# Attention scores half a key tile ahead, in the beats in which layer 1 has no step in flight

## The chip, the cores and the metric

The kernel runs on one core of a Trainium2 chip, as one launch. The metric is the device time of that launch in microseconds. The kernel before took 4408.22 us, the median of three runs (4399.3, 4408.22 and 4410.45).

## What is computed

Two layers of attention over a graph of N = 2048 nodes with F = 256 features, for a batch of B = 8, all in fp32. Layer 0 is four-headed attention (head size 64) in which the scores are clipped to ±10, an edge that is missing counts as -10, and the softmax is taken over each chunk of 256 keys on its own and the chunks' results are added. Layer 1 is a graph attention layer of one head over the layer-0 output. Both are followed by a residual sum and a layer normalisation. Cut to what matters here:

```python
scores = einsum('bhnd,bhjcd->bhnjc', q, kc) / sqrt(Dh)      # layer 0
scores = clip(scores, -10.0, 10.0)
scores = where(mask == 0, -10.0, scores)
attn = softmax(scores, axis=-1)                             # over the 256 keys of a chunk
ctx = einsum('bhnjc,bhjcd->bhnd', attn, vc)
out = ctx @ Wo.T + bo
...
e = leaky_relu(s_i[:, :, None] + s_j[:, None, :], 0.2)      # layer 1
e = where(mask, e, -inf)
h_prime = softmax(e, axis=-1) @ Wh
```

## The kernel before

**Beats.** The program is one long list of beats, and each engine gets its instructions in the order in which the beats write them down; nothing reorders them afterwards. For each batch element b there are four blocks of 512 queries (ib), and for each block 16 key tiles of 128 (c). One beat is one key tile of one block, so there are 16 × 4 × 8 = 512 beats, and behind them a tail in which layer 1 of the last batch element finishes. Two beats are a chunk (J counts chunks; half is 0 or 1 in it).

**What a beat holds for layer 0 (lines 880 to 978).** The two head pairs (hp 0 and 1) each get a score tile `sc` of 128 keys × 2 heads × 512 queries, that is 4 KB in each partition, or two banks of PSUM. TensorE writes both (line 904), VectorE clips both against the mask in place (line 914), ScalarE takes the exponential of both into SBUF tiles `e` (line 917), which sets the place in PSUM free. Then comes the product with the values for the chunk before (`prev`): the sums of the softmax ("part 2", with a matrix of ones) and the first half of each head's values ("part 0") in the beat of half 0, the second half ("part 1") in the beat of half 1 (line 933). Each part goes to a place of 2 KB, `m`, from which ScalarE copies it to SBUF: `ds` (line 947) for the sums, `un` (line 941) for the values. From `ds` a transfer makes a small tile `dc`, VectorE takes its reciprocal (line 955), two more transfers spread it to `r`, VectorE multiplies (lines 966 and 968) and GpSimd adds into `ctxT` (line 969).

**What surrounds it.** `begin_beat` writes ScalarE's and VectorE's part of layer 1, `end_beat` its product on TensorE (line 746) and then one step of each of the generators in flight: the projections, the masks (in the first batch element alone: lines 154 to 161 and 201), the end of a layer-0 block (`fin`: the product `po`, two normalisations, the transposes `pt`), the preparation of layer 1 (`prelude`: `pw`, `psj`, the row maxima at line 438, the transposes `pab`), and the end of a layer-1 block (`fin1`). After the beat c = 15 the next block's queries are projected (`pq`, line 256).

**PSUM.** Three pools fill its 16 KB in each partition: `ps_s` has two places of 4 KB (tag `sc`), `ps_u` has one of 4 KB, which holds layer 1's sums (`us`), and `ps_m` has two of 2 KB, tag `m`, which all the short-lived tiles share in turn: `m` of the value products, `pk`, `pv`, `pq`, `po`, `pt`, `pw`, `psj`, `pab`. A tile that takes a place waits until what held it before has been read.

**Where layer 1 rests.** Layer 1 of a batch element can only start when layer 0 of that element is done, and takes fewer beats than layer 0. So there is a stretch in each batch element without any step of layer 1. With `b`, `ib` and `c` counted through, these are the beats 0 to 88, and then 19 beats (from c = 6 of the first block to c = 8 of the second) of each of the elements 2 to 7, from 134, 198, 262, 326, 390 and 454 on: 203 of 512 beats. The name `spare` (line 898) tells of them. In these beats each third score tile goes into the place of `ps_u`, so that scores have three places in turn; in all other beats they have the two of `ps_s`.

Of the kernel before, what the change touches and what calls it, by code (L numbers as in the profile page):

```python
# [9 lines left out]
F32 = mybir.dt.float32  # L10
# [3 lines left out]
AF = mybir.ActivationFunctionType  # L14
# [5 lines left out]
P = 128  # L20
CLIP = 10.0
# [7 lines left out]
def tile_adj_attention__then__gat(  # L29
# [108 lines left out]
    def mask_block(n, ib, hf, name):  # L138
        t = two.tile([P, HT, IB], I8, tag=f"mask{n}", name=f"mk{n}_{name}")
        nc.sync.dma_start(out=t, in_=mask[n][ib, hf])  # L140
        return t
# [21 lines left out]
    def masks_made():  # L163


        for ib in range(NIB):
            for hf in range(2):
                first = (ib, hf) == (0, 0)
                while not first and beat < HT * (2 * ib + hf - 1):
                    yield  # L170
                if first:
                    raw, m0 = first_raw, first_m0
                else:
                    raw = one.tile([P, HT, IB], I32, tag="wh", name=f"raw{ib}_{hf}")
                    m0 = two.tile([P, HT, IB], I8, tag="mask0", name=f"mk0_0_{ib}_{hf}")
                    blocks0[ib, hf] = m0
                m1 = two.tile([P, HT, IB], I8, tag="mask1", name=f"mb1_{ib}_{hf}")
                for i in range(HT // 2 + 2):
                    if first:
                        if 0 < i < HT // 2:  # L180
                            make_mask(0, m0, raw, ib, hf, 2 * i, 2)
                    elif i < HT // 2:
                        load_raw(raw, ib, hf, 2 * i, 2)
                    if i >= 2:
                        if not first:
                            make_mask(0, m0, raw, ib, hf, 2 * i - 4, 2)
                        make_mask(1, m1, raw, ib, hf, 2 * i - 4, 2)
                    if i or not first:
                        yield
                nc.sync.dma_start(out=mask[0][ib, hf], in_=m0)  # L190
                nc.sync.dma_start(out=mask[1][ib, hf], in_=m1)
# [667 lines left out]


    first_m0 = two.tile([P, HT, IB], I8, tag="mask0", name="mk0_0_0_0")
    blocks0 = {(0, 0): first_m0}
    make_kT(0, 0)
    make_mask(0, first_m0, first_raw, 0, 0, 0, 2)
    qT = make_qT(0, 0, xT_kv[0, 0])
# [4 lines left out]

    prev = None
    halves_done = 0
    mk0 = {}
    for J in range(total + 1):
        b, ib, j = J // (NIB * NCH), J // NCH % NIB, J % NCH
        live = J < total
# [3 lines left out]
        for half in range(2):  # L880
            c = 2 * j + half
            if live:

                if c % HT == 0:
                    if b == 0:
                        mk = blocks0[ib, c // HT]
                    else:
                        mk = mk0.pop((b, ib, c // HT))
                if c % HT == 1:
                    n = (b * NIB + ib) * 2 + c // HT + 1  # L890
                    nb, nib, nhf = n // (2 * NIB), n // 2 % NIB, n % 2
                    if 0 < nb < B:
                        mk0[nb, nib, nhf] = mask_block(0, nib, nhf, f"{nb}_{nib}_{nhf}")
            begin_beat(RATE if b < B - 1 else LAST_RATE)
            if live:
                scs = []

                spare = not (l1_open() or leaking)
                for hp in range(NPAIR):
                    pool, tag = (ps_u, "us") if spare and halves_done % 3 == 2 else (ps_s, "sc")  # L900
                    halves_done += 1
                    sc = pool.tile([P, 2, IB], F32, tag=tag, name=f"sc{b}_{ib}_{c}_{hp}")
                    for h in range(2):
                        nc.tensor.matmul(  # L904
                            sc[:, h, :],
                            kTs[b][c // TPB][h * D : (h + 1) * D, hp, ts(c % TPB, P)],
                            qT[h * D : (h + 1) * D, hp, :],
                            start=True,
                            stop=True,
                        )  # L910
                    scs.append(sc)
                cap = mk[:, c % HT, :].unsqueeze(1).to_broadcast([P, 2, IB])
                for hp in range(NPAIR):
                    nc.vector.scalar_tensor_tensor(scs[hp], scs[hp], -CLIP, cap, ALU.max, ALU.min)  # L914
                for hp in range(NPAIR):
                    e = eight.tile([P, 2, IB], F32, tag="e", name=f"e{b}_{ib}_{c}_{hp}")
                    nc.scalar.activation(e, scs[hp], AF.Exp)  # L917
                    cur["es"].append(e)
            middle_of_beat()

            early = J < NIB * NCH
            if prev is not None:
                if half == 0:

                    pool, tag = (one, "hr") if early and J % 3 == 2 else (two, "un")
                    prev["un"] = pool.tile([P, 2, IB], F32, tag=tag, name=f"un{prev['name']}")
                for part in ((2, 0), (1,))[half]:
                    m = ps_m.tile([P, IB], F32, tag="m", name=f"u{prev['name']}_{part}")
                    for i in range(2):
                        pc = 2 * prev["j"] + i  # L930
                        for h in range(H):
                            f0 = h * D + part * DH
                            nc.tensor.matmul(  # L933
                                m[h * DH : (h + 1) * DH, :],
                                prev["v"][pc // TPB][:, pc % TPB, f0 : f0 + DH] if part < 2 else ones[:, 0:DH],
                                prev["es"][2 * i + h // 2][:, h % 2, :],
                                start=(i == 0),
                                stop=(i == 1),
                            )
                    if part < 2:  # L940
                        nc.scalar.copy(prev["un"][:, part, :], m)  # L941
                    else:

                        ds = two.tile([P, IB], F32, tag="ds", name=f"ds{prev['name']}")
                        nc.scalar.copy(ds, m)  # L947
                        dc = two.tile([P, IB // DH], F32, tag="dc", name=f"dc{prev['name']}")
                        nc.sync.dma_start(
                            out=dc, in_=ds.rearrange("(h m) (n w) -> h m n w", m=DH, n=DH)[:, 0, :, :]  # L950
                        )
                        prev["dc"] = dc

                        def inverse(p=prev):
                            nc.vector.reciprocal(p["dc"], p["dc"])  # L955
                            p["rd"] = dram3.tile([H, IB], F32, tag="rd", name=f"rd{p['name']}")
                            nc.sync.dma_start(out=p["rd"].rearrange("h (m w) -> (h m) w", m=DH), in_=p["dc"])

                        def spread(p=prev):
                            p["r"] = two.tile([P, IB], F32, tag="r", name=f"r{p['name']}")  # L960
                            nc.sync.dma_start(out=p["r"], in_=p["rd"].unsqueeze(1).to_broadcast([H, DH, IB]))

                        def scaled(p=prev):
                            r2 = p["r"].unsqueeze(1).to_broadcast([P, 2, IB])
                            if p["j"] == 0:
                                nc.vector.tensor_mul(p["ctxT"], p["un"], r2)
                            else:
                                nc.vector.tensor_mul(p["un"], p["un"], r2)  # L968
                                nc.gpsimd.tensor_add(p["ctxT"], p["ctxT"], p["un"])  # L969
                            if p["j"] == NCH - 1:  # L970
                                ctx_done[p["b"], p["ib"]] = beat
                            if p["j"] == NCH - 3:
                                fins.append(fin(p["b"], p["ib"], p["ctxT"]))

                        lag = 1 if early else 0
                        at(beat + lag, inverse)
                        at(beat + lag, spread)
                        at(beat + 2 + 2 * lag, scaled)

            end_beat()  # L980
            if half == 1:

                if live and j == NCH - 2 and J + 2 < total:
                    nb, nib = (b, ib + 1) if ib + 1 < NIB else (b + 1, 0)
                    xq = xT_tile(nb, nib, "q")
                if live and j == NCH - 1 and J + 1 < total:
                    qT = make_qT(nb, nib, xq)
            beat += 1
# [51 lines left out]
```

## Time and profile before

The profile is that of one execution, which took 4410.7 us; the span of its instructions is 4408.9 us.

| | |
|---|---|
| median of three runs | 4408.22 us |
| the profiled execution, and its span | 4410.7 us, 4408.9 us |
| mean granted TensorE clock | 0.976 |
| busy: TensorE, VectorE, ScalarE, GpSimd | 92%, 77%, 58%, 40% |
| score matmuls (line 904) | 1049.1 us over 4096 |
| clip (line 914) | 1206.8 us over 1024, 1222 ns each |
| exponential (line 917) | 1035.2 us over 1024, 1021 ns each |
| value products (line 933), values and sums | 984.8 us and 497.0 us |
| copies `un` and `ds` (lines 941 and 947) | 587 ns and 580 ns each |

How to read the profile: for each instruction it has the start, the time it took, the engine, the line of the code, what it writes and reads (out<-in), and how long the engine had been idle before it and which instruction ended that idle time. A TensorE instruction has two rows, the load of its weights (PEld) and the matmul itself (PE); a score or value matmul in fp32 shows as two. Where a group of instructions of one kind is merged, the time is that of the whole group and the idle time that before its first.

### The profile page before, as it was taken

To read this page: it belongs to the slowest core of one execution; us is meant where nothing else is said; L and a number is where in the kernel's file an instruction comes from. 1 tells how busy PE (TensorE), PEld (TensorE's weight loads), DVE (VectorE), ACT (ScalarE), POOL (GpSimd) and SP (SyncE) were. 2 spreads that over 40 slices of the span, in tenths; PEclk is the share of its full clock that TensorE was granted. 3 is DMA by queue.
4 is the path that set the end of the run, shared out by engine and by line. 5 is a ranking of instruction groups with operands and counts; after the bars stand their busy time and mean duration, and the time that the engine had idled before them with its cause. 6 is when DMAs were issued, how large, how long until landed. Compare 5 with 4: busy or idle time off the path is not lost. (4 is left out here: it accounts for less than half of the span.)

```text
span 4408.9 us, 61096 instructions
## 1 busy us (share of the span) xinstructions
PE 4071.0 (92%) x23053; PEld 1917.2 (43%) x23053; DVE 3414.9 (77%) x4530; ACT 2563.4 (58%) x3842; POOL 1762.7 (40%) x901
## 2 busy tenths in 40 slices
PE   8889989999899999999899998999989999899767
PEld 3223334454344533444344543445434454344456
DVE  5876589965898659986699766996579965888777
ACT  5655556665566556665556655566556665555546
POOL 0222235542455434444245442554325542355420
PEclk9999999999999999999999999999999999999889
DMA  5554232222322233321333223222232222322321
GB/s 162 171 173 143 78 109 90 80 75 85 102 88 82 64 106 96 98 77 51 105 100 104 73 72 106 82 93 81 70 104 85 90 76 66 116 79 80 125 75 58
DMA packets 257641, 415.62 MB, mean 94 GB/s; under 512 B 85441, under 2 KB 120513, under 8 KB 256449
## 3 DMA queue, kind: packets, MB, share of 16 engines
q1 hardware_dynamic: 257344, 411.71, 30.7%
q8 instruction: 181, 2.97, 0.3%
q14 instruction: 116, 0.94, 0.1%
HBM read 340.66 MB, written 68.88 MB: 93 GB/s over the span
## 5 line engine op out<-in xcount | busy, mean ns | idle before, releaser
L917 ACT ACTIVATE e<-sc 128x1024 f32<-128x1024 f32 x1024 | 1035.2, 1021 | 1059.5 <-DVE sc L914 1018.0
L914 DVE SCALAR_TENSOR_TENSOR sc<-sc,mk 128x1024 f32<-128x1024 f32 x1024 | 1206.8, 1222 | 545.4 <-PE sc L904 357.5
L904 PE MATMUL sc<-qT,kT 64*128 64x512 f32 x4096 | 1049.1, 628 | 61.8 <-ACT e L917 58.5
L969 POOL TENSOR_TENSOR ctxT<-ctxT,un 128x1024 f32<-128x1024 f32 x224 | 569.3, 2542 | 1169.1 <-DVE un L968 1032.0
L933 PE MATMUL u<-e,v 128*32 128x512 f32 x8192 | 984.8, 598 | 3.3 <-ACT ds L947 3.2
L746 PE MATMUL us<-wh,w 128*128 128x256 f32 x3584 | 880.0, 395 | 83.2 <-ACT w L727 60.2
L746 PEld LDWEIGHTS us<-wh,w 128*128 128x128 f32 x3584 | 667.7, 193 | 425.0 <-ACT w L727 111.7
L736 POOL TENSOR_TENSOR acc<-acc,w 128x512 f32<-128x512 f32 x392 | 602.0, 1536 | 544.9 <-ACT w L727 534.3
L904 PEld LDWEIGHTS sc<-qT,kT 64*128 64x128 f32 x4096 | 349.1, 189 | 574.0 <-issue 369.0
L718 DVE SCALAR_TENSOR_TENSOR w<-ab,sj,w 128x512 f32<-128x512 f32 x512 | 571.7, 1138 | 6.2 <-ACT w L714 6.2
L933 PEld LDWEIGHTS u<-e,v 128*32 128x32 f32 x8192 | 240.6, 110 | 665.7 <-issue 541.5
L933 PE MATMUL u<-e,ones 128*32 128x512 f32 x4096 | 497.0, 603 | 0.0
L723 DVE TENSOR_TENSOR w<-w,mk 128x512 f32<-128x512 f32 x512 | 458.0, 915 | 38.3 <-DMA mk<-mask 35.7
L438 DVE CUSTOM_DVE_ANT_0 fb<-sj_row,fb 128x1024 bf16<-128x1024 f32 x240 | 381.8, 1601 | 4.2 <-DMA fb<-far 4.2
L714 ACT ACTIVATE w<-ab,sj 128x512 f32<-128x512 f32 x512 | 352.1, 714 | 10.2 <-POOL acc L734 5.4
L727 ACT ACTIVATE w<-w 128x512 f32<-128x512 f32 x512 | 308.8, 629 | 76.8 <-DVE w L723 76.4
L941 ACT COPY un<-u 128x512 f32<-128x512 f32 x512 | 300.8, 587 | 66.4 <-PE u L933 58.3
L968 DVE TENSOR_TENSOR un<-un,r 128x1024 f32<-128x1024 f32 x224 | 277.4, 1239 | 45.0 <-DMA r<-rd 44.8
L933 PEld LDWEIGHTS u<-e,ones 128*32 128x32 f32 x4096 | 107.5, 110 | 353.8 <-issue 300.5
L955 DVE RECIPROCAL dc<-dc 128x16 f32<-128x16 f32 x256 | 63.6, 249 | 156.6 <-DMA dc<-ds 141.1
L357 PE MATMUL po<-WT_o,ctxT 128*128 128x256 f32 x512 | 121.6, 391 | 30.6 <-POOL ctxT L969 23.2
L947 ACT COPY ds<-u 128x512 f32<-128x512 f32 x256 | 148.5, 580 | 1.6 <-PE u L933 1.6
(112 smaller groups left out, 3097.7 us busy)
## 6 DMA issues: line engine op xcount, KB each, us to landing
r<-rd SPq DMA_DIRECT2D x256, 256.0 KB
mk<-mask SPq DMA_DIRECT2D x120, 512.0 KB
fb<-far SPq DMA_DIRECT2D x240, 256.0 KB
xT_k<-in_xT_dram SPq DMA_DIRECT2D x32, 512.0 KB
raw<-in_adjT_dram SPq DMA_DIRECT2D x32, 512.0 KB
rawf<-in_adj_dram SPq DMA_DIRECT2D x32, 512.0 KB
x<-in_x_dram SPq DMA_DIRECT2D x32, 512.0 KB
h_d<-y SPq DMA_DIRECT2D x32, 512.0 KB
```

The costliest lines, as they stand in the source:

```text
L438: nc.vector.tensor_tensor_reduce(out=fb, in0=row, in1=fb, scale=1.0, scalar=2 * FAR * 0.999, op0=ALU.add, op1=ALU.max, accum_out=dst,)
L714: nc.scalar.activation(self.w, k["ab"][:, 1, :], AF.Identity, bias=k["sj"][:, 1, c : c + 1])
L718: nc.vector.scalar_tensor_tensor(self.w, k["ab"][:, 0, :], k["sj"][:, 0, c : c + 1], self.w, ALU.add, ALU.max)
L723: nc.vector.tensor_tensor(self.w, self.w, self.k["mks"][self.c // HT][:, self.c % HT, :], ALU.min)
L727: nc.scalar.activation(self.w, self.w, AF.Exp)
L736: nc.gpsimd.tensor_add(k["acc"], k["acc"], self.w)
L746: nc.tensor.matmul(k["us"][:, t, :], self.w[:, ts(t, P)], k["wh"][c // TPB][:, c % TPB, 0:F], start=(first and t % 2 == 0), stop=last, ski ...
L904: nc.tensor.matmul(sc[:, h, :], kTs[b][c // TPB][h * D : (h + 1) * D, hp, ts(c % TPB, P)], qT[h * D : (h + 1) * D, hp, :], start=True, sto ...
L914: nc.vector.scalar_tensor_tensor(scs[hp], scs[hp], -CLIP, cap, ALU.max, ALU.min)
L917: nc.scalar.activation(e, scs[hp], AF.Exp)
L933: nc.tensor.matmul(m[h * DH : (h + 1) * DH, :], prev["v"][pc // TPB][:, pc % TPB, f0 : f0 + DH] if part < 2 else ones[:, 0:DH], prev["es"] ...
L969: nc.gpsimd.tensor_add(p["ctxT"], p["ctxT"], p["un"])
```

## The change

In a beat in which layer 1 rests, the scores written are no longer those of the two head pairs of tile c, but the second head pair of tile c and the first of tile c + 1. Their clips follow in that order. Of the exponentials, that of (c, 0), whose score was clipped in the beat before, is written at the head of the beat, ahead of `begin_beat`; that of (c, 1) follows the clips; that of (c + 1, 0) is left for the next beat. A block's first tile has nothing ahead, so the beat c = 0 writes three scores and three clips, and c = 15 one of each. The same holds where a rest begins (three) and behind its end (one), and at one tile of the very first block (c = 7 to 8), whose mask is made only just before. The masks of layer 0 are looked up by tile in one table instead of being fetched once in half a block. The number of matmuls, clips, exponentials and transfers is unchanged, and so are the three places and the rule that hands them out.

```diff
-                for hp in range(NPAIR):
-                    pool, tag = (ps_u, "us") if spare and halves_done % 3 == 2 else (ps_s, "sc")
-                    halves_done += 1
-                    sc = pool.tile([P, 2, IB], F32, tag=tag, name=f"sc{b}_{ib}_{c}_{hp}")
...
-                    scs.append(sc)
-                cap = mk[:, c % HT, :].unsqueeze(1).to_broadcast([P, 2, IB])
-                for hp in range(NPAIR):
-                    nc.vector.scalar_tensor_tensor(scs[hp], scs[hp], -CLIP, cap, ALU.max, ALU.min)
-                for hp in range(NPAIR):
-                    e = eight.tile([P, 2, IB], F32, tag="e", name=f"e{b}_{ib}_{c}_{hp}")
-                    nc.scalar.activation(e, scs[hp], AF.Exp)
-                    cur["es"].append(e)
+    def scores(n, hp):
+        nonlocal halves_done
+        pool, tag = (ps_u, "us") if spare and halves_done % 3 == 2 else (ps_s, "sc")
+        halves_done += 1
+        sc = pool.tile([P, 2, IB], F32, tag=tag, name=f"sc{b}_{ib}_{n}_{hp}")
...
+        return sc
+
+    def clip(sc, n):
+        cap = blocks0[b, ib, n // HT][:, n % HT, :].unsqueeze(1).to_broadcast([P, 2, IB])
+        nc.vector.scalar_tensor_tensor(sc, sc, -CLIP, cap, ALU.max, ALU.min)
+
+    def exponentials(chunk, n, hp, sc):
+        e = eight.tile([P, 2, IB], F32, tag="e", name=f"e{b}_{ib}_{n}_{hp}")
+        nc.scalar.activation(e, sc, AF.Exp)
+        chunk["es"].append(e)
...
+            if ahead_sc is not None:
+                exponentials(cur, c, 0, ahead_sc)
             begin_beat(RATE if b < B - 1 else LAST_RATE)
             if live:
...
                 spare = not (l1_open() or leaking)
+                todo = [(c, hp) for hp in range(0 if ahead_sc is None else 1, NPAIR)]
+                if spare and c + 1 < NT and (b, ib, c + 1) != (0, 0, HT):
+                    todo.append((c + 1, 0))
+                scs = [scores(n, hp) for n, hp in todo]
+                for (n, hp), sc in zip(todo, scs):
+                    clip(sc, n)
+                ahead_sc = None
+                for (n, hp), sc in zip(todo, scs):
+                    if n == c:
+                        exponentials(cur, c, hp, sc)
+                    else:
+                        ahead_sc = sc
             middle_of_beat()
```

More of the change, by code (lines that the diff above doesn't have):

```diff
@@ L175, in masks_made @@
                     m0 = two.tile([P, HT, IB], I8, tag="mask0", name=f"mk0_0_{ib}_{hf}")
-                    blocks0[ib, hf] = m0
+                    blocks0[0, ib, hf] = m0
                 m1 = two.tile([P, HT, IB], I8, tag="mask1", name=f"mb1_{ib}_{hf}")
@@ L861, in tile_adj_attention__then__gat @@
     first_m0 = two.tile([P, HT, IB], I8, tag="mask0", name="mk0_0_0_0")
-    blocks0 = {(0, 0): first_m0}
+    blocks0 = {(0, 0, 0): first_m0}
     make_kT(0, 0)
@@ L872, in tile_adj_attention__then__gat @@
     halves_done = 0
-    mk0 = {}
+    ahead_sc = None
[4 more added lines that the diff above has]
+        sc = pool.tile([P, 2, IB], F32, tag=tag, name=f"sc{b}_{ib}_{n}_{hp}")
+        for h in range(2):
+            nc.tensor.matmul(
+                sc[:, h, :],
+                kTs[b][n // TPB][h * D : (h + 1) * D, hp, ts(n % TPB, P)],
+                qT[h * D : (h + 1) * D, hp, :],
+                start=True,
+                stop=True,
+            )
+        return sc
[6 more added lines that the diff above has]
+        chunk["es"].append(e)
     for J in range(total + 1):
@@ L882, in tile_adj_attention__then__gat @@
             if live:
[L884 to L888, printed above, removed]
                 if c % HT == 1:
@@ L892, in tile_adj_attention__then__gat @@
                     if 0 < nb < B:
-                        mk0[nb, nib, nhf] = mask_block(0, nib, nhf, f"{nb}_{nib}_{nhf}")
+                        blocks0[nb, nib, nhf] = mask_block(0, nib, nhf, f"{nb}_{nib}_{nhf}")
+            if ahead_sc is not None:
+                exponentials(cur, c, 0, ahead_sc)
             begin_beat(RATE if b < B - 1 else LAST_RATE)
             if live:
-                scs = []
                 spare = not (l1_open() or leaking)
-                for hp in range(NPAIR):
-                    pool, tag = (ps_u, "us") if spare and halves_done % 3 == 2 else (ps_s, "sc")
-                    halves_done += 1
-                    sc = pool.tile([P, 2, IB], F32, tag=tag, name=f"sc{b}_{ib}_{c}_{hp}")
[L903 to L910, printed above, removed]
-                    scs.append(sc)
-                cap = mk[:, c % HT, :].unsqueeze(1).to_broadcast([P, 2, IB])
-                for hp in range(NPAIR):
-                    nc.vector.scalar_tensor_tensor(scs[hp], scs[hp], -CLIP, cap, ALU.max, ALU.min)
-                for hp in range(NPAIR):
-                    e = eight.tile([P, 2, IB], F32, tag="e", name=f"e{b}_{ib}_{c}_{hp}")
-                    nc.scalar.activation(e, scs[hp], AF.Exp)
-                    cur["es"].append(e)
+                todo = [(c, hp) for hp in range(0 if ahead_sc is None else 1, NPAIR)]
[4 more added lines that the diff above has]
+                    clip(sc, n)
+                ahead_sc = None
+                for (n, hp), sc in zip(todo, scs):
[3 more added lines that the diff above has]
+                        ahead_sc = sc
             middle_of_beat()
```

## The prediction, made before the changed kernel was run

> **What bounds the kernel now.** I read the page first: the busy line, then the 40 slices.
>
> ```profile
> PE 4071.0 (92%) x23053; PEld 1917.2 (43%) x23053; DVE 3414.9 (77%) x4530; ACT 2563.4 (58%) x3842; POOL 1762.7 (40%) x901
> PE   8889989999899999999899998999989999899767
> DVE  5876589965898659986699766996579965888777
> PEclk9999999999999999999999999999999999999889
> ```
>
> TensorE (PE) sets the end; where VectorE's digits fall to 5 and 6, PE's fall to 8: these are the rests of layer 1. Second view: busy time by stretch, cut at the beats' first scores. The first line is batch element 0 and the start of 1, the second one later rest, the third a stretch with layer 1 in it (length, then PE, PEld, DVE, ACT, POOL busy, clock).
>
> ```profile
> 18.00:622.00 604.00, 542.72 (x3209) 194.17 (x3207) 425.03 (x539) 334.30 (x446) 155.00 (x66) 0.96 0.44 137
> 1020.00:1153.00 133.00, 119.94 (x734) 46.25 (x734) 87.32 (x129) 74.33 (x115) 43.14 (x20) 0.97 0.35 107
> ...
> 627.00:1020.00 393.00, 379.34 (x2131) 190.09 (x2129) 325.29 (x411) 237.89 (x360) 190.47 (x101) 1.00 0.27 79
> ```
>
> All seven rests together last 1410 us, of which PE is busy 1267: 143 us of idle time are all there is to win directly. A rest beat takes 7.0 us (133 / 19). Third view: the timeline of one rest, PE's gaps one by one. They stand at the same tiles in every batch element. The kind that matters, twice:
>
> ```profile
> 1054.48 2.33 DVE L914 SCALAR_TENSOR_TENSOR sc<-sc,mk 128x1024 f32<-128x1024 f32 x2
> 1055.72 2.15 ACT L917 ACTIVATE e<-sc 128x1024 f32<-128x1024 f32 x2 [3.62 <-DVE sc L914]
> 1057.77 0.58 ACT L941 COPY un<-u 128x512 f32<-128x512 f32 x1
> 1058.40 4.57 PE L398 MATMUL pw<-W_aug,hTl 128*128 128x258 f32 x12 [1.87 <-ACT un L941]
> ...
> 1136.41 2.36 DVE L914 SCALAR_TENSOR_TENSOR sc<-sc,mk 128x1024 f32<-128x1024 f32 x2
> 1137.67 2.16 ACT L917 ACTIVATE e<-sc 128x1024 f32<-128x1024 f32 x2 [3.31 <-DVE sc L914]
> 1139.72 0.58 ACT L947 COPY ds<-u 128x512 f32<-128x512 f32 x1
> 1140.36 0.27 PE L461 MATMUL pab<-ident,m 128*8 128x128 f32 x1 [2.84 <-ACT ds L947]
> ```
>
> PE wants a 2 KB place. The copy that frees it was ready long before, but stands on ScalarE behind both exponentials, and these wait for a clip that VectorE makes late. Two other kinds, a score that waits for a score place, and a copy behind a busy ScalarE:
>
> ```profile
> 1109.50 2.35 DVE L914 SCALAR_TENSOR_TENSOR sc<-sc,mk 128x1024 f32<-128x1024 f32 x2
> 1110.75 2.15 ACT L917 ACTIVATE e<-sc 128x1024 f32<-128x1024 f32 x2 [4.82 <-DVE sc L914]
> 1111.83 1.13 PE L904 MATMUL sc<-qT,kT 64*128 64x512 f32 x4 [1.14 <-ACT e L917]
> ...
> 1033.03 2.08 ACT L329 ACTIVATE y<-y,nmr_b,rstd_b 128x256 f32<-128x256 f32 x4
> 1035.01 1.93 ACT L917 ACTIVATE e<-sc 128x1024 f32<-128x1024 f32 x2
> 1036.81 0.60 ACT L947 COPY ds<-u 128x512 f32<-128x512 f32 x1
> 1037.55 1.06 PE L383 MATMUL pt<-ident,y 128*128 128x128 f32 x8 [1.02 <-ACT ds L947]
> ```
>
> And what a long gap costs afterwards, behind the 2.84 us at `pab`:
>
> ```profile
> 1140.56 3.39 PE L904 MATMUL sc<-qT,kT 64*128 64x512 f32 x8
> 1141.00:1144.50 3.50, 3.50 (x12) 0.89 (x12) 2.98 (x5) 0.93 (x1) 3.33 (x2) 0.51 0.05 6
> ```
>
> Eight score matmuls take 3.39 us, elsewhere 1.99: the clock was 0.51.
>
> **What the Trainium skill says.** "TensorE: Matmul & The Clock Gate", Part 1: TensorE's clock falls to one half after an idle window of a free-running 3413 ns. The trace's clock records agree on the length, 3.41 us or multiples, but it falls already after gaps of 1.9 to 2.9 us; and after some of 2.3 to 3.5 us it doesn't. The measurement decides. "Perfetto Trace Analysis", Identifying Performance Opportunities: consistent bubbles, the same gap repeating, can mean too little PSUM; the `pab` gap is 2.84, 2.91, 2.88, 2.80, 2.84 and 2.91 us in the six later rests. "PSUM — Partial Sum Buffer", Specifications: eight banks of 2 KiB in a partition. The pools take all (2 × 4 + 4 + 2 × 2 KB), so the change has only the order to work with.
>
> **The change, part by part.** It adds and removes no instruction; TensorE's work stays, so all it can win is gaps.
>
> (1) *The copies on ScalarE.* Call D the start of a beat's first clip. Before: first exponential at D + 1.26, second to D + 3.42, then the copy. After: the first clip is that of (c, 1), whose exponential is the only one between clip and copy, D + 1.26 to D + 2.28. That of (c, 0) stands at the head of the beat, where ScalarE idles anyway (1.7 to 3.6 us before most exponentials). Copies come 1.02 us earlier, one exponential, wherever VectorE is late. Per later rest: `pw` (1.87 to 3.26 us) 1.02, `pab` 1.02, `pq` (1.64 us behind `un`) 0.95. `po` (1.1 to 3.7 us) waits for GpSimd's `ctxT` behind VectorE's row maxima: nothing, and it swallows the 0.48 of a value product just ahead. `pt` (1.02): in the lines above ScalarE didn't wait for the clip; both exponentials stand between the normalisation and `ds`, as after the change: nothing. 3.0 per rest.
>
> (2) *The score places.* The gap at L904 is for the exponential of (c-1, 0), D + 2.28 of the beat before. After the change PE has written (c, 1) by then and wants a place for (c+1, 0), which the exponential of (c-1, 1) frees: again D + 2.28. Equal; none of these gaps (14 us in the later rests, 27 in the first two elements) goes. If clipping ahead of VectorE's long work lets PE pass after all, some half of the 41 us would go; below nothing, see the slow case.
>
> (3) *Block starts.* At c = 0 three scores (3 × 1.0 us) stand ahead of the value products, so `ds`, `dc` and the reciprocal (1.9 us behind the copy in the trace) come up to 1 us later, and VectorE's clip of c = 1 stands behind that reciprocal. From there VectorE is busy without a break to the `pab` gap. I charge 0.5 per rest (0 to 1.0).
>
> So a later rest wins 2.5 us, and so does the rest part of element 1, with the same gaps: 7 × 2.5 = 17.5. Element 0, from its timeline: `pk` 1.0 at 32 us, `pv` 0.5 at 49 and 1.0 at 78 (there the third score fills the gap), `pq` 1.0 at 123, `po` 1.0 at 165. Later gains there end in gaps that VectorE's mask work (2.2 to 5.3 us at L904) or the `xT_q` transfer (2.4 and 2.7) sets: 0. Together 4.5, in all 22.
>
> (4) *The clock.* About 16 half-clock windows of 3.41 us stand behind gaps that shrink; each costs half, 1.7 us (measured above: 1.4 at the scores, 0.2 at the product behind). Were all avoided, 27 us; none, 0. A `pab` gap of 1.8 can still trip it, as the `pw` gap of 1.87 did, so I take rather less than half: 10.
>
> Head of the queue: the exponential moved ahead of `begin_beat` passes no layer-1 work but in the single beat behind each rest. SP's and POOL's queues keep their order. Sum: 22 + 10 = 32, from the profiled 4410.7 to 4379. The median shown is 2.5 lower than that execution, so 4376 to 4379; I say 4378.
>
> **Rivals.**
> *The score gaps shrink too* (half of 41, with their nine clock windows half gone, 8): 4378 - 28 = 4350. For it: VectorE then has one clip done before its long work. Against it: part (2).
> *Gains are swallowed* by the next gap that VectorE, GpSimd or a transfer sets, as the 0.48 is by `po`: only pieces that VectorE answers by waiting for PE remain. `pq` and little clock, 7 × 1 = 7: 4404. For it: VectorE's unbroken stretch of 40 us in each rest. Against it: behind it VectorE does wait for PE (0.52 and 0.61 us after `pab`, 7.33 after `pw`).
> *Slower: the second score of a beat now waits for (c-1, 1), on ScalarE one exponential behind (c-1, 0).* Where ScalarE and not VectorE is late, a place comes 1.02 us later. A rest has five groups of four scaling instructions of 2.1 us in all on ScalarE, element 0 some eight: 7 × 5 + 8 = 43 beats, 44 us if each is exposed, against the 22: 4432. It decides from about 35 exposed beats. Against it: ScalarE waited for the clip 17 times in a rest's 19 beats, and PE usually has time over. I see one such beat per rest (1132 us, 0.6 more), which the `pab` gap takes up.
>
> **How the numbers follow.** Likeliest 0.60, 4378, own range 4360 to 4394; score gaps too 0.16, 4350; swallowed 0.15, 4404; slower 0.09, 4432. What can be told from no change is 0.3%, 13 us: faster is below 4395, slower above 4421. Faster 0.76, within 0.15, slower 0.09. The range 4345 to 4408 leaves out the slower case and the ends of the second.
>
> **What would show it.** Right: `pab` gaps near 1.8 us, `pq` near 0.7, `pw` 1 us shorter, `pt`, `po` and the score gaps as before, one exponential between clip and copy, fewer half-clock windows, beats with layer 1 at their old 8.9 us. Wrong: score gaps growing in many beats, or PE's gaps moved from `pab` and `pw` to the next tile without the rests getting shorter.

## The result, and the profile after

The changed kernel takes 4389.84 us (median of six runs, 4386.54 to 4391.84), the kernel before 4406.41 us (six runs, 4398.81 to 4410.45). The ratio is 0.9964 [0.9951, 0.9977]: 16.6 us faster, 0.36%. The forecast was 4378, with 4360 to 4394 as its own range: 30 us under the 4408.22 known then, of which somewhat over half came.

The profiled executions are further apart. That of after took 4386.54 us, the shortest of its six, with a span of 4384.7 us; that of before, 4410.7, is the longest of its six. So the traces differ by 24.2 us where the medians differ by 16.6, and everything read from the two traces below overstates the gain by some 8 us.

First view: the busy line of the page of after.

```profile
PE 4055.8 (92%) x23053; PEld 1913.0 (44%) x23053; DVE 3417.1 (78%) x4530; ACT 2555.5 (58%) x3842; POOL 1759.3 (40%) x901
```

TensorE does the same 23053 matmuls in 15.2 us less busy time (4071.0 before), while the other engines' sums hardly move. No work was taken out, so this is the clock: its mean went from 0.976 to 0.979, and the trace's clock records have 215.0 us at half speed before and 184.3 us after, 30.7 us less, which at half speed is 15.3 us. The other 9 us of the 24 are idle time of TensorE.

To see where, I cut both traces at the first scores of the same tiles. "First block" is c = 6 to 15 of a later rest, "second block" c = 0 to 9 behind it; both are sums over the six rests.

| stretch | us before | us after | PE idle, before to after | half clock, before to after |
|---|---|---|---|---|
| element 0 | 431.4 | 426.1 | 44.1 to 40.6 | 37.5 to 34.1 |
| rest of element 1 | 179.9 | 173.9 | 17.3 to 13.2 | 10.2 to 6.8 |
| first blocks | 448.3 | 425.6 | 32.7 to 17.8 | 20.5 to 3.4 |
| second blocks | 378.6 | 381.5 | 48.8 to 58.6 | 37.5 to 23.9 |
| beats with layer 1 | 2678.4 | 2685.9 | 107.4 to 110.7 | 27.3 to 34.1 |
| tail | 276.8 | 276.4 | 81.9 to 82.3 | 79.9 to 79.9 |

The first blocks are 22.7 us shorter, and element 0 and the rest of element 1 another 11.3. The second blocks and the beats with layer 1 behind them give 10.4 us back. Second view: the busy time of each engine in the first rest's two stretches and summed over six rests, after (length, then PE, PEld, DVE, ACT, POOL with counts, clock, DMA share, GB/s; the two sums are those of the first and of the second blocks).

```profile
1009.63:1080.03 70.40, 67.88 (x410) 28.46 (x410) 36.46 (x55) 43.78 (x70) 20.64 (x10) 1.00 0.32 98
...
sum 425.64, PE 407.85 PEld 172.28 DVE 219.18 ACT 260.00 POOL 122.64; mean PE 67.98 PEld 28.71 DVE 36.53 ACT 43.33 POOL 20.44
...
1080.03:1141.74 61.71, 52.01 (x346) 17.21 (x346) 54.92 (x78) 32.52 (x48) 23.57 (x10) 1.00 0.42 129
...
sum 381.47, PE 322.87 PEld 107.97 DVE 326.83 ACT 195.21 POOL 139.94; mean PE 53.81 PEld 17.99 DVE 54.47 ACT 32.53 POOL 23.32
```

The two stretches are different places: in the first VectorE is busy 219.2 of 425.6 us and TensorE 407.9; in the second VectorE, with the row maxima, 326.8 of 381.5 and TensorE only 322.9. The second blocks of before, where TensorE was busy 7 us longer because of its clock, were 3 us shorter all the same:

```profile
sum 378.56, PE 329.75 PEld 109.59 DVE 324.17 ACT 201.30 POOL 140.06; mean PE 54.96 PEld 18.27 DVE 54.03 ACT 33.55 POOL 23.34
```

Third view: the timeline of after at the tiles that the prediction showed, `pw`, `pq` and `pab` of element 2.

```profile
1044.61 2.33 DVE L893 SCALAR_TENSOR_TENSOR sc<-sc,mk 128x1024 f32<-128x1024 f32 x2
1045.85 1.02 ACT L897 ACTIVATE e<-sc 128x1024 f32<-128x1024 f32 x1 [2.48 <-DVE sc L893]
1046.77 0.58 ACT L956 COPY un<-u 128x512 f32<-128x512 f32 x1
1047.40 2.88 PE L398 MATMUL pw<-W_aug,hTl 128*128 128x258 f32 x12 [0.53 <-ACT un L956]
...
1076.40 3.70 PE L256 MATMUL pq<-xT_q,WT_q 128*128 128x512 f32 x8 [0.88 <-ACT un L956]
...
1123.06 2.35 DVE L893 SCALAR_TENSOR_TENSOR sc<-sc,mk 128x1024 f32<-128x1024 f32 x2
1124.32 1.02 ACT L897 ACTIVATE e<-sc 128x1024 f32<-128x1024 f32 x1 [3.14 <-DVE sc L893]
1125.23 0.58 ACT L962 COPY ds<-u 128x512 f32<-128x512 f32 x1
1125.87 0.27 PE L461 MATMUL pab<-ident,m 128*8 128x128 f32 x1 [1.34 <-ACT ds L962]
1126.07 1.99 PE L882 MATMUL sc<-qT,kT 64*128 64x512 f32 x8
```

One exponential stands between the clip and the copy, not two. The gap at `pw` is 0.53 us where it was 1.87, at `pq` 0.88 where it was 1.64, at `pab` 1.34 where it was 2.84, and the eight scores behind `pab` take 1.99 us again where they took 3.39. The line of `pq` in before:

```profile
1091.19 3.70 PE L256 MATMUL pq<-xT_q,WT_q 128*128 128x512 f32 x8 [1.64 <-ACT un L941]
```

Over the six rests the longest wait of each tile sums to 6.6 us at `pw` (14.6 before), 5.3 at `pq` (9.8) and 8.0 at `pab` (17.2).

Fourth view: what is new in the same timeline. First the place at which `pt` waited in the first block, then the single beat of the second block in which ScalarE is late, then the end of the rest.

```profile
1022.05 2.04 PE L882 MATMUL sc<-qT,kT 64*128 64x512 f32 x8 [0.76 <-ACT e L897]
...
1117.87 1.91 ACT L897 ACTIVATE e<-sc 128x1024 f32<-128x1024 f32 x2
1118.92 2.04 PE L882 MATMUL sc<-qT,kT 64*128 64x512 f32 x8 [1.50 <-ACT e L897]
...
1133.33 2.07 ACT L329 ACTIVATE y<-y,nmr_b,rstd_b 128x256 f32<-128x256 f32 x4 [1.64 <-DVE nmr_b L327]
1135.31 1.91 ACT L897 ACTIVATE e<-sc 128x1024 f32<-128x1024 f32 x2
1137.12 0.57 ACT L962 COPY ds<-u 128x512 f32<-128x512 f32 x1
1137.83 1.06 PE L383 MATMUL pt<-ident,y 128*128 128x128 f32 x8 [1.86 <-ACT ds L962]
```

The 1.02 us of `pt` in the first block are gone, and a score waits 0.76 us in its place. The other two are losses: 0.97 has become 1.50 at the score, and `pt` of the second block, which didn't wait before, waits 1.86 us for a copy that stands behind the scaling of the normalisation (2.07 us, and itself late by VectorE's `nmr_b`) and two exponentials. VectorE's part of that normalisation, and `pt`, in before, and then VectorE's part in after:

```profile
1144.06 1.23 DVE L914 SCALAR_TENSOR_TENSOR sc<-sc,mk 128x1024 f32<-128x1024 f32 x1 [0.52 <-PE sc L904]
1145.20 1.32 DVE L438 CUSTOM_DVE_ANT_0 fb<-sj_row,fb 128x1024 bf16<-128x1024 f32 x1
...
1146.45 0.15 DVE L327 SCALAR_TENSOR_TENSOR nmr_b<-mv_b,rstd_b 128x4 f32<-128x4 f32 x1
...
1151.46 0.66 PE L383 MATMUL pt<-ident,y 128*128 128x128 f32 x4
```

```profile
1131.20 1.95 DVE L438 CUSTOM_DVE_ANT_0 fb<-sj_row,fb 128x1024 bf16<-128x1024 f32 x1
...
1133.09 0.15 DVE L327 SCALAR_TENSOR_TENSOR nmr_b<-mv_b,rstd_b 128x4 f32<-128x4 f32 x1
```

From the clip ahead of `pab` (1136.41 before, 1123.06 after) to `nmr_b` it is 10.0 us in both kernels, and so in all six rests. In before VectorE waited 0.52 us for a score on that way; in after it doesn't, but the row maximum takes 1.95 us instead of 1.32. Why that one takes longer is not shown.

Fifth view: the first product of layer 1 behind the rest of element 3, after, and then the same two instructions in before.

```profile
1680.72 1.29 DVE L723 TENSOR_TENSOR w<-w,mk 128x512 f32<-128x512 f32 x2 [5.87 <-DMA mk<-mask]
1682.13 5.41 PE L746 MATMUL us<-wh,w 128*128 128x256 f32 x16 [2.42 <-ACT w L727]
1687.46 2.08 PE L882 MATMUL sc<-qT,kT 64*128 64x512 f32 x8
```

```profile
1695.98 1.29 DVE L723 TENSOR_TENSOR w<-w,mk 128x512 f32<-128x512 f32 x2 [4.88 <-DMA mk<-mask]
1697.38 3.72 PE L746 MATMUL us<-wh,w 128*128 128x256 f32 x16 [1.43 <-ACT w L727]
1702.54 2.26 PE L904 MATMUL sc<-qT,kT 64*128 64x512 f32 x8 [1.44 <-ACT e L917]
```

VectorE waits for the transfer of layer 1's first mask in both kernels. Relative to that transfer TensorE comes there a microsecond earlier in after: it waits 2.42 us instead of 1.43, and then does its 16 products at half clock, 5.41 us instead of 3.72. Little of these 1.69 us is lost, for in before the scores behind the product wait another 1.44 us. The product comes to half clock in three of the seven rests in after and in none in before; the seven waits at it sum to 14.9 us, 9.1 before.

### The profile page after: what moved, and what is told of

It is laid out like the page before. It is cut to its first block, busy times and chain, and to the rows that moved or that the text cites. A ratio compares the mean times of both kernels' runs of the same rounds, so it can differ in the third digit from the quotient of the medians.

```text
span 4384.7 us, 61166 instructions
## 1 busy us (share of the span) xinstructions
PE 4055.8 (92%) x23053; PEld 1913.0 (44%) x23053; DVE 3417.1 (78%) x4530; ACT 2555.5 (58%) x3842; POOL 1759.3 (40%) x901
## 3 DMA queue, kind: packets, MB, share of 16 engines
q1 hardware_dynamic: 257344, 411.71, 30.7%
## 4 chain that ended last, share of the span: by engine, by line
PE 57%; DVE 23%; ACT 7%; DMA 7%; issue 5%; POOL 1%; SPq 0%; DVEq 0%; ACTq 0%; POOLq 0%
PE u L948 17%; PE sc L882 14%; PE us L746 12%; DVE sc L893 6%; DVE fb L438 3%; DVE w L718 3%; PE pv L275 3%; PE pk L256 3%; ACT e L897 3%; DMA dc<-ds 2%; PE pq L256 2%; DVE w L723 2%; PE po L357 2%; PE pw L398 2%; PE us L761 1%
## 5 line engine op out<-in xcount | busy, mean ns | idle before, releaser
L882 PE MATMUL sc<-qT,kT 64*128 64x512 f32 x4096 | 1038.7, 622 | 71.8 <-ACT e L897 68.6
```

The source lines that it names most:

```text
L882: nc.tensor.matmul(sc[:, h, :], kTs[b][n // TPB][h * D : (h + 1) * D, hp, ts(n % TPB, P)], qT[h * D : (h + 1) * D, hp, :], start=True, sto ...
```

## The experiments

Two questions: whether ScalarE's order is what wins, and why the second half of a rest gives some of it back. Stretch sums below are each from one profiled execution; second blocks and beats with layer 1 are taken together where the cut between them moves (3057.0 us before, 3067.4 after).

**The exponential not moved.** The change with the exponential of (c + 1, 0) written in the beat of its clip, behind that of (c, 1), not left to the next beat.

```diff
-        chunk["es"].append(e)
+        return e
...
-                exponentials(cur, c, 0, ahead_sc)
+                cur["es"].append(ahead_sc)
...
+                    e = exponentials(cur, n, hp, sc)
                     if n == c:
-                        exponentials(cur, c, hp, sc)
+                        cur["es"].append(e)
                     else:
-                        ahead_sc = sc
+                        ahead_sc = e
```

> TensorE's and VectorE's half tile ahead is kept, but ScalarE takes the exponential of (c+1, 0) in the same beat, so that two exponentials stand ahead of the copies again. Theory A (the gain is that of the copies, one exponential earlier): it goes, 4400 to 4410 us, with the pab gap back near 2.8 us and the pw gap near 2.4. Theory B (the gain is the half tile ahead on TensorE and VectorE, whatever ScalarE's order): it stays, 4385 to 4393 us.

4415.1 us (4411.84 to 4419.57) beside 4402.66 of before, ratio 1.003 [1.0019, 1.004]: slightly slower than before, and 5 us above what I had put down for it. The timeline of this kernel at `pab`:

```profile
1137.33 2.35 DVE L893 SCALAR_TENSOR_TENSOR sc<-sc,mk 128x1024 f32<-128x1024 f32 x2
1138.59 2.15 ACT L897 ACTIVATE e<-sc 128x1024 f32<-128x1024 f32 x2 [3.23 <-DVE sc L893]
1140.64 0.58 ACT L963 COPY ds<-u 128x512 f32<-128x512 f32 x1
1141.28 0.38 PE L461 MATMUL pab<-ident,m 128*8 128x128 f32 x1 [2.83 <-ACT ds L963]
```

Two exponentials are back between clip and copy, and with them the gap of before: 2.83 us (2.84). So with ScalarE's order undone no gain of the half tile ahead is left. The extra loss of 12 us is not explained. One possible cause is this edit's own: an exponential written that early wants one of eight `e` buffers, which in odd beats the same beat's value product has still to free. But the profile shows only two waits of that kind, 2.5 us in all.

**ScalarE's order alone.** The kernel before, its scores and clips as they were, with the exponential of (c, 1) left to the head of the next beat while layer 1 rests.

```diff
+            if late is not None:
+                late()
+                late = None
             begin_beat(RATE if b < B - 1 else LAST_RATE)
...
-                for hp in range(NPAIR):
-                    e = eight.tile([P, 2, IB], F32, tag="e", name=f"e{b}_{ib}_{c}_{hp}")
-                    nc.scalar.activation(e, scs[hp], AF.Exp)
-                    cur["es"].append(e)
...
+                exponential(0, scs[0])
+                if spare:
+                    late = lambda sc=scs[1], f=exponential: f(1, sc)
+                else:
+                    exponential(1, scs[1])
```

> The order of the kernel before on TensorE and VectorE (both scores and clips of tile c in beat c), but in a rest the exponential of (c, 1) is left to the head of the next beat, so that one exponential stands ahead of the copies. Theory A: the whole gain, 4380 to 4391 us, rather below the changed kernel since a block's first beat keeps two scores. Theory B: no gain, 4403 to 4410 us.

4392.46 us (4384.39 to 4400.34), ratio 0.9977 [0.9968, 0.9987]: 10 us faster than before, and 1.5 us above what theory A had put down. Its timeline at `pq` and `pab`:

```profile
1075.38 3.70 PE L256 MATMUL pq<-xT_q,WT_q 128*128 128x512 f32 x8 [0.50 <-ACT un L952]
...
1121.98 1.02 ACT L922 ACTIVATE e<-sc 128x1024 f32<-128x1024 f32 x1 [3.14 <-DVE sc L918]
1122.90 0.58 ACT L958 COPY ds<-u 128x512 f32<-128x512 f32 x1
...
1123.53 0.27 PE L461 MATMUL pab<-ident,m 128*8 128x128 f32 x1 [1.33 <-ACT ds L958]
```

The gap at `pab` is that of the change (1.33), the one at `pq` is shorter still (0.50), and the first blocks take 428.6 us, 19.7 us less than before, where the change has 22.7 less. Behind them it gives back as much as the change (3068.4), but in another place: its second blocks are 19.9 us longer than before and its beats with layer 1 8.5 us shorter. With the run before, this shows that the order on ScalarE makes most of the change's gain. Whether the half tile ahead on TensorE and VectorE adds to it is not settled, since the intervals of the two ratios overlap.

**Look-ahead in the first block of a rest only,** and **no third score at a block's start.**

```diff
-                if spare and c + 1 < NT and (b, ib, c + 1) != (0, 0, HT):
+                if spare and (b == 0 or ib == 0) and c + 1 < NT and (b, ib, c + 1) != (0, 0, HT):
```

> The changed kernel, but from element 1 on it looks ahead only in the first block of a rest (up to c = 15), and works as before in the second (c = 0 to 8). Theory A1 (the second block is bound by VectorE and ScalarE; what the pab gap gives back is swallowed there, and the third score at c = 0 and the later places cost 1.6 us per rest): 8 to 12 us below the changed kernel, 4378 to 4383 us. Rival A2 (the pab gain is real and kept): 7 x (1.5 us + some clock) = 10 to 18 us above it, 4400 to 4408 us. Nothing either way: 4388 to 4392 us, the gap just moves.

```diff
-                if spare and c + 1 < NT and (b, ib, c + 1) != (0, 0, HT):
+                if spare and 0 < c < NT - 1 and (b, ib, c + 1) != (0, 0, HT):
```

> The changed kernel, but with two scores in a block's first beat (c = 0) and three in its second (c = 1). If the third score at c = 0 delays the sums, their transfer and VectorE's reciprocal by up to 1 us per block start: 12 block starts, 5 to 10 us below the changed kernel, 4380 to 4385 us. If that time is covered: 4388 to 4392 us. If the third score at c = 1, in the shorter kind of beat, costs more there: above 4393 us.

4387.42 us (4378.12 to 4391.25), 0.9960 [0.9948, 0.9973], and 4388.02 us (4379.53 to 4396.97), 0.9966 [0.9953, 0.9978]. Neither can be told from the change. For the first kernel A1 and A2 both missed, and the third case, that nothing happens either way, is the nearest; for the second the time of the third score is covered, and nothing of it can be measured. Without any look-ahead in its second block the first kernel gives back 8.9 us all the same (3065.9), so the new waits of the fourth view can't be the whole reason.

**Look-ahead in the second block only.**

```diff
-                if spare and c + 1 < NT and (b, ib, c + 1) != (0, 0, HT):
+                if spare and b > 1 and ib == 1 and c + 1 < NT:
```

> The kernel before, but looking ahead in the second block of the rests of elements 2 to 7 alone (c = 0 to 8). If what the pab gap wins is swallowed behind it (A1): 4399 to 4408 us, the time of the kernel before. If it is kept, as the prediction had it: 6 x (1.0 + 0.8 - 0.5) = 8 us or more below, 4388 to 4396 us.

4413.33 us (4408.28 to 4427.7) beside 4408.2, ratio 1.0015 [1.0007, 1.0024]: slightly slower than before, and above even the 4399 to 4408 of A1. The second blocks do get shorter, 372.6 us, though `pt` waits 1.87 us in each rest here too; but the beats with layer 1 behind them take 2687.0, 8.6 more, of which 51.2 us are at half clock (27.3 before). What the second block wins is lost again behind the rest.

**Short row maxima, before and after.** The row maxima are taken over a quarter of the keys, which leaves out three quarters of that part of the computation; everything else is as in the kernel before and in the change.

```diff
-                half_max(sj_row[:, ts(n % 2, HN)], fbs.pop(0), m2[:, n % 2, n // 2 : n // 2 + 1])
+                fb = fbs.pop(0)
+                half_max(sj_row[:, n % 2 * HN : n % 2 * HN + HN // 4], fb[:, : HN // 4], m2[:, n % 2, n // 2 : n // 2 + 1])
```

> The kernel before with VectorE's row maxima for layer 1 (line 438, elements 0 to 6) taken over a quarter of the keys: part of the computation left out, to make VectorE light in the second block of each rest. Only its difference to the next run counts. By itself: 5 to 25 us below the kernel before, since the gaps at c = 3 (scores, po) shrink.

> The changed kernel with the same row maxima over a quarter of the keys. If VectorE's load in the second block is what takes back the gain there (theory A1), the difference to the run before it is 24 to 32 us, near the predicted 32. If it isn't, the difference is that of the full kernels, 12 to 19 us.

4352.41 us (4343.84 to 4356.91) and 4321.06 us (4316.14 to 4327.67), ratios 0.987 [0.9857, 0.9884] and 0.9802 [0.9789, 0.9815]. By themselves the short maxima are worth 55.8 us, not the 5 to 25 put down. The change is now worth 31.3 us instead of 16.6, within the 24 to 32 of A1. The intervals of the ratios leave some 8 us of doubt on the 31 and some 6 on the 17, so they are apart, but not by an exact amount. The two profiled executions are only 25.1 us apart (4343.84 and 4318.73), hardly more than the 24.2 of the full kernels, so their stretches say less than the medians. The second blocks, summed as above, of before and of after with short maxima:

```profile
sum 367.86, PE 323.61 PEld 108.98 DVE 276.19 ACT 199.57 POOL 132.14; mean PE 53.94 PEld 18.16 DVE 46.03 ACT 33.26 POOL 22.02
```

```profile
sum 358.43, PE 319.80 PEld 108.78 DVE 274.73 ACT 195.07 POOL 130.28; mean PE 53.30 PEld 18.13 DVE 45.79 ACT 32.51 POOL 21.71
```

With 50 us less work on VectorE the change shortens the second blocks by 9.4 us, where with the full maxima it lengthened them by 2.9, and second blocks and layer 1 together give nothing back (3001.6 and 3000.7). The beats with layer 1 alone are again 8.6 us longer (2633.7 and 2642.3), much as with the full maxima. So the runs point to the row maxima as what takes back the gain in the second blocks, but not behind them. Whether it is the time that they take on VectorE, or the chain of transfers in which they stand, is not separated; and they reach beyond the second blocks, since in the kernel before they shorten the beats with layer 1 by 44.7 us.

**The order alone in element 0, the look-ahead from element 1 on.**

```diff
+            if late is not None:
+                exponentials(*late)
+                late = None
...
-                if spare and c + 1 < NT and (b, ib, c + 1) != (0, 0, HT):
+                if spare and b > 0 and c + 1 < NT:
                     todo.append((c + 1, 0))
...
-                    if n == c:
+                    if n == c and hp == 1 and b == 0:
+                        late = cur, c, hp, sc
+                    elif n == c:
                         exponentials(cur, c, hp, sc)
```

> The changed kernel, but in element 0, where the masks are made, with the order of the late exponential instead of the half tile ahead. The trace of that order had element 0 3.5 us shorter. Expected 4383 to 4388 us against 4388 to 4391 of the changed kernel; if the profile's 3.5 us were chance, the same as the changed kernel.

4389.71 us (4378.51 to 4392.15), 0.9952 [0.994, 0.9964]; not told apart from the change, and above the 4383 to 4388 put down. Element 0 takes 423.1 us in its profile (426.1 in the change), but 3 us can't be told in the times.

**Layer 1's first mask a beat earlier,** in the change, in the kernel before and in the last version. The fifth view suggested that the wait for this mask is where the gain goes.

```diff
+                mks = []
                 while ib not in st["ab"] or beat < st["ab"][ib][0]:
+                    if ib == 0 and ib in st["ab"] and not mks:
+                        mks = [mask_block(1, ib, 0, f"{b}_{ib}_0")]
                     yield None
-                mks = [mask_block(1, ib, 0, f"{b}_{ib}_0")]
+                if not mks:
+                    mks = [mask_block(1, ib, 0, f"{b}_{ib}_0")]
```

> The changed kernel, with the first mask of each layer-1 pass loaded one beat (some 7 us) earlier. Theory M: the changed kernel's TensorE reaches layer 1's first product 1 us sooner, but waits there 2.4 instead of 1.4 us for weights whose mask has not landed, and half the time trips the half clock; with the mask there in time this is kept: 4368 to 4378 us, and 20 to 26 us below the next run. Rival: VectorE's work around it takes the time anyway, 4382 to 4390 us and 12 to 19 us below the next run.

> The kernel before with the same earlier load. Theory M: only its own gap of 1.4 us at seven places goes, 4394 to 4401 us. Rival: 4402 to 4410 us, no change.

> The late exponential in element 0, the half tile ahead in the later rests, and the earlier load: 4364 to 4376 us by theory M, the same as the first of these three if element 0 makes no difference; by the rival 4380 to 4390 us.

Beside 4403.77: 4367.98 us (4365.66 to 4374.71), 0.9918 [0.9901, 0.9935]; 4384.47 us (4374.95 to 4389.73), 0.9953 [0.9937, 0.9969]; 4364.74 us (4360.17 to 4372.44), 0.9911 [0.9895, 0.9926]. The kernel before with the earlier mask, at the same place of its timeline:

```profile
1680.58 1.28 DVE L727 TENSOR_TENSOR w<-w,mk 128x512 f32<-128x512 f32 x2
...
1685.45 3.72 PE L750 MATMUL us<-wh,w 128*128 128x256 f32 x16
```

Neither instruction waits any longer. But the mask gains 19 us in before too, which neither forecast had (theory M 4394 to 4401), and the two kernels are still 16.5 us apart, as without it; the change without the earlier load was not run beside them, but by the ratios (0.9964 and 0.9918) it gains some 20. Theory M wanted the two 20 to 26 apart, its rival 12 to 19. The intervals leave some 10 us of doubt on the 16.5, so the theory is not excluded, but nothing speaks for it beyond the times of the first and the last kernel, which it had right, the first at the very edge of its range: the wait for the mask looks like a loss of its own, which both kernels have, and not like the place where the change's gain goes. The last of the three is the fastest kernel of the study that does the whole computation, 39 us or 0.9% under before, though it can't be told from the first.

## Why the prediction was right, and where it was not

**What bounds the kernel, and the order on ScalarE (step 1): right.** The gaps shrank because one exponential and not two stands ahead of the copies, and the two runs on ScalarE's order show it from both sides: with the order alone the gain is 10 us (the whole change has 17), with everything but the order none is left. "Perfetto Trace Analysis", Identifying Performance Opportunities, in the Trainium skill reads consistent bubbles as perhaps too little PSUM. The trace here agrees only in form: places were short at `pab`, but no place was added, and 2.84 became 1.34 us when the engine that empties them did so one instruction earlier. Per later rest `pw` gained 1.33 (forecast 1.02), `pq` 0.75 (0.95), `pab` 1.53 (1.02), and the first block's idle time fell by 14.9 / 6 = 2.5 us where `pw` and `pq` made 2.0 of the forecast.

**"A later rest wins 2.5 us": the step that failed.** The first block alone won that; the sum counted `pab` on top, as if its microsecond reached the end of the rest. The gap shrank, but the second blocks' idle time rose from 48.8 to 58.6 us. I had seen VectorE's unbroken stretch there, held it against the swallowing rival that VectorE waits for TensorE behind `pab`, and concluded that the gain passes. It doesn't, as the run with the second block alone shows, and the runs with short maxima point the same way. Per later rest 2.5 us of idle time went in the first block and 9.8 / 6 = 1.6 came back in the second: 0.9 us and not 2.5. (The rest of element 1 won 4.1 us of idle time where 2.5 were forecast, element 0 won 3.5 where 4.5 were.) The likeliest case and the rival "gains are swallowed" are both half right: passed on in the first block, swallowed in the second. From the six rests' first blocks 22.7 us came, and 10.4 went. The measured 4389.84 lies about midway between the two, 12 us above the 4378 and 14 below the 4404 of the rival; that it falls into the range owes something to the range's width, and to the clock (step 4).

How it is taken back shows best behind `pab` (all figures are means of six rests). Counted from the clip ahead of it, `pab` comes 1.13 us earlier in the change (2.81 us where it was 3.94), but `pt`, which needs the normalisation that VectorE reaches 10.0 us behind that clip in both kernels, comes only 0.14 us earlier (14.78 and 14.92): what TensorE wins at `pab` it waits for at `pt`.

Ahead of `pab` it is less clear. From `psj`, behind which layer 1's key rows are fetched and the row maxima begin, to `pab` it is 52.48 us in before and 52.49 in the change (means of six rests again), as if a chain of fixed length ran there; with short maxima it is 50.63 and 49.45. With ScalarE's order alone it is 50.53, but that kernel loses the time behind `pab`: in each rest a value product waits 2.13 us for an exponential that stands behind the scaling of the same normalisation. From `psj` to layer 1's first product every kernel with the full maxima and the mask as it was takes 79.4 to 80.5 us, none less than before; with short maxima it is 77.26 and 76.49. An earlier start of the key rows was not tried, so what sets this length stays open.

**`pt`, "nothing", and the score places, "equal" (steps 1 and 2): not quite.** The score gaps did not go, as forecast, but they grew: TensorE's idle time ahead of scores is 71.8 us in the page of after and 61.8 in that of before. So the mechanism of the rival that ends slower exists, at a fraction of its 44 us: a score waits 0.76 us where `pt` waited 1.02, and 0.53 us longer in the second block. Missed altogether was the end of the rest, where ScalarE is late by a normalisation: `pt` 1.86 us in each of six rests. These 11 us are more than the whole rise of idle time in the second blocks.

**The third score at a block's start (step 3): no cost.** Charged 0.5 us per rest; the run without it can't be told from the change.

**The clock (step 4): right in kind, mis-sized.** Of about 16 windows that could go, nine of 3.41 us went (30.7 us in all): 15 us and not 10. In the sum this covered for the missing idle time, 9 us and not 22: 24 between the traces where 32 were forecast.

**"Beats with layer 1 at their old 8.9 us": wrong by 7.5 us,** of which half clock makes 6.8 / 2 = 3.4 and idle time 3.3, at layer 1's first product among others (fifth view). Their instructions are unchanged, but at their start TensorE now comes earlier than the mask's transfer allows: 5.8 us more of waiting there over the seven rests, against which the waits of 1.44 us behind it are gone in three.

## What to carry to other kernels

Where a matmul waits for PSUM, look first at what stands ahead of the emptying copy on its engine: here one exponential moved out of its way (left to the head of the next beat, where the engine idles anyway) was worth 0.2% in this kernel without touching the matmuls. Sum such gains by stretch, each with its own bound, and stop counting where another engine is busy for most of it: here the same microsecond passed on where VectorE was busy half the time and was lost where it was busy 86% of it. And look at what waits at the end of the stretch for something with a time of its own; there a load one beat earlier gave as much as the whole change.

## What was not expected of the hardware

The clock falls to one half after short gaps, so that a gap of 2 to 3 us can make the matmuls behind it longer by 1.4 to 1.7 us: 16 products took 5.41 us behind a gap of 2.42 us and 3.72 behind one of 1.43, and eight scores 3.39 and 1.99 behind the gaps of 2.84 and 1.34 at `pab`. "TensorE: Matmul & The Clock Gate", Part 1, of the Trainium skill speaks of an idle window of 3413 ns; the length of the half-clock stretches agrees (3.41 us or multiples), the gap that it takes does not. Yet it isn't the length of the gap alone: behind 1.87 us at `pw` the clock fell in before, and behind 2.44 and 3.68 us at `po` (elements 2 and 3) it didn't. What decides was not tried. So the worth of a gap can't be told from its length: between the two profiled executions 9 us of idle time came with 15 us of clock.

The size of the mask's gain was another surprise. Expected from a gap of 1.43 us, the earlier load was put at 4394 to 4401 us for the kernel before and gave 4384.47: in its profile the wait of 1.44 us at the score behind that product is gone too. Over the seven rests the two waits sum to 9.1 and 10.1 us, 19.2 in all, of which 0.6 is left: that is the size of the gain. The beats with layer 1 take 2656.5 us instead of 2678.4.
